# Two graph-convolution layers on one core: z2's operands ahead of one sum, and one sum behind the last multiplication

## The chip, the cores and the metric

The kernel runs on one core of one Trainium2 chip. The metric is the device time of the whole program in microseconds (us); lower is better. Engines are named TensorE (PE, its weight loads PEld), VectorE (DVE), ScalarE (ACT), GpSimd (POOL) and SyncE (SP). L423 is line 423 of the kernel before.

## The reference, cut to what matters

Eight batches of 2048 nodes with 64 features go through two residual graph layers over one adjacency matrix `adj`. Layer 0 has weights of each node's own, made from a 16-wide embedding:

```python
w = einsum('nd,dkio->nkio', embedding, weight)        # D = 16, K = 3
b = einsum('nd,do->no', embedding, bias)
As = [I, A, 2 A @ A - I]
x_g = einsum('knm,bmc->bnkc', stack(As), x)
out = einsum('bnki,nkio->bno', x_g, w) + b
x = layernorm(x + out)
```

Layer 1 uses powers of the same matrix with one weight for all nodes, `x = layernorm(x + concat(x, Ax, (2AA-I)x, ...) @ W + bias)`. All inputs and outputs are float32.

## The kernel before, in words

**Stages.** `pattern` treats `adj` as a pattern of zeros times a factor per row. Two hops of layer 0 come first (`hop_x`, then `seven_products`, which does a block product in seven instead of eight half-size products). They leave z0 (the features), z1 (one hop) and z2 (two hops), each as 16 tiles of 128 nodes by 512 columns (8 batches of 64 features). Then comes the stage of the change: the loop of L897 over the 16 tiles, in which layer 0's node-wise weights are applied. Behind it `run(third + ...)` (L1097) does layer 1's hops.

**One tile of layer 0.** `mix0` (L412) makes eight *pieces*, (u, h) for u in 0 to 3 (a pair of batches) and h in 0 and 1 (half of the 16 embedding dimensions). `product` gives each piece 18 matmuls (L423) into one double bank of PSUM: three inputs (z0, z1, z2) times three operand parts, on two halves of the rows. Each of the inputs is split into three float32r operands: "high" (a ScalarE copy, L327), "low" (source minus high, VectorE L329), and a third, mixed one (VectorE L332 when `quick`, else ScalarE L334 and GpSimd L335). z2's operands of the *following* tile are made by `of_second` in this tile: its first `next` is high, the second low, the third the mixed operand.

The product of a piece must then be multiplied by the node's embedding values and summed over the 8 dimensions of its half. There are three ways:
- kind "D": VectorE multiplies out of PSUM (L439) into `aside`, of which there is one buffer; a VectorE sum over it (L468) follows later as ("reduce", u, h);
- kind "R": ScalarE multiplies in eight steps (L452), and VectorE sums as ("reduce", u, h);
- kind "P": ScalarE multiplies, and GpSimd adds in three steps (L457, "sum") and once more (L461, "add").

("add_reduced", h, us) is GpSimd's addition of finished sums to the tile (L472). A piece's double bank comes free when its multiplications are done.

**The order.** From L751 on, VectorE, ScalarE and GpSimd run in the order in which the program writes their instructions (`ordered`). That order is written out by hand: `at[n]` lists what is issued ahead of piece n, and `pieces` says which piece is of which kind. In tiles 0 to 14 the pieces are

```python
pieces = [(2, 0, "R"), (0, 1, "D"), (3, 0, "R"), (0, 0, "P"), (1, 1, "D"), (1, 0, "P"), (2, 1, "D"), (3, 1, "D")]
```

Into the same lists go the norm of the tile before (`scaled_to_unit`, L374: squares on ScalarE L368, sum on VectorE L379, five small GpSimd steps L385 to L389 and the scaling L390), the transpositions of the next z1 tile ("pt") and of the last h ("pt", copied by L321), and, after the pieces, the projection of the tile before (`project`, L485: matmuls "pu" L493, ScalarE copies L502).

**PSUM.** `bank` hands out four double banks under one tag, for pieces, transpositions, projections and, behind the last tile, for the four accumulators "accT" of layer 1's first hop (L691). By the addresses in the compiled program of before, the first piece of a tile gets the bank of the last tile's piece (2,1), and the transposition behind it that of piece (3,1). Of the accumulators, the first product's two get the banks of the last tile's pieces (2,1) and (3,1).

**The last tile** has another order. It also prepares layer 1's first steps by `early`: `y_high` is a ScalarE copy (L249), `y_low` a VectorE subtraction (L253), `operands` a ScalarE copy of the matrix part (L684).

Of the kernel before, what the change touches and what calls it, by code (L numbers as in the profile page):

```python
# [41 lines left out]
def pattern(  # L42
# [275 lines left out]
    def transpose(src, tag, pt=None):  # L318

        tt = xcpool.tile([P, B // 2, P], F32, tag="ln_xc", name=tag)  # L320
        ordered(nc.scalar.copy(by_half(tt), transposed(src, pt)))  # L321
        return tt
# [83 lines left out]
    def begin_sum(t):  # L406
        ordered(nc.gpsimd.tensor_tensor(bc(0, t), bc(0, t), ebias[:, t : t + 1, :].to_broadcast([P, B, C]), ALU.add))
# [77 lines left out]
    def project(t, hT, pus=None):  # L485


        for g in range(2):
            pm = bank("pu") if pus is None else pus[g]
            for i in range(2):  # L490
                for j in range(2):
                    q = slice(j * C, (j + 1) * C)
                    nc.tensor.matmul(  # L493
                        pm[:, j, i * 3 * C : (i + 1) * 3 * C], lhsT=hT[q, 2 * g + i, :], rhs=v[q],
                        start=True, stop=True,
                    )
            got = pm[:, :, : 6 * C].rearrange("p j (i k c) -> p j i k c", i=2, k=3)

            order = ["p (i j) c -> p j i c", "p (j i) c -> p j i c", "p (j i) c -> p j i c"]
            to = [bc(k, t)[:, 4 * g : 4 * g + 4, :].rearrange(order[k], j=2) for k in range(3)]  # L500
            for k in range(3):
                ordered(nc.scalar.copy(to[k], got[:, :, :, 2 - k, :]))  # L502
# [242 lines left out]
    def times_r(t):  # L745
        to = z2[:, t, :].rearrange("p (j n) -> p j n", n=P)
        r = rrow[:, t * P : (t + 1) * P].unsqueeze(1).to_broadcast([P, B // 2, P])
        ordered(nc.gpsimd.tensor_tensor(to, to, r, ALU.mult))
# [9 lines left out]
    def operands(t, quick=False):  # L758

        xt = work2.tile([P, B // 2, P], F32, tag="t0", name="xt")  # L760
        load(nc.sync, xt, xT[t])
        tt = [None] * 3

        def begin(k, src, quick):
            where, tag = ((rawp, "raw"), (spool, "s"))[k != 2]
            high = hpool.tile([P, B // 2, P], F32R, tag="hl", name="hl")
            pair = where.tile([P, 2, B // 2, P], F32R, tag=tag, name="parts")
            tt[k] = [high, pair[:, 0], pair[:, 1]]
            return parts(src, tt[k], by_half if k == 1 else lambda to: to, quick)

        def of_x():
            yield from begin(0, xt, True)

        def of_hop(pt=None):
            yield from begin(1, transposed(z[1][t], pt), quick)

        def of_second():
            yield from begin(2, by_pair(z[2][t]), True)

        return tt, of_x(), of_hop, of_second()  # L780
# [100 lines left out]
    def early(i, *kinds):  # L881

        got = third_got.setdefault(i, {})
        for lead, part in sorted(third[i], key=lambda part: -part[0]):
            if part.__name__ in kinds:
                part(got)
        third[i] = [part for part in third[i] if part[1].__name__ not in kinds]

    def go(it):
        return lambda: next(it)  # L890
# [5 lines left out]
    everything = range(B // 2)  # L896
    for t in range(NT):  # L897
        got, last = {}, t == NT - 1
        at = [[] for _ in range(9)]
        n1, n2, root, n3 = [lambda: next(norm)] * 4 if t else [nothing] * 4  # L900

        if not last:
            following, of_x, of_hop, of_second = coming
            of_hop = of_hop()
            at[1] += [go(of_x)] * (1 if t else 3)
            at[1] += [n1, lambda: begin_sum(t + 1)]
            if t + 2 < NT:
                at[1] += [lambda: times_r(t + 2)]
            at[1] += [go(of_hop)]
            at[2] += [("reduce", 0, 1), n2, go(of_hop), go(of_hop), ("reduce", 2, 0)]  # L910
            at[3] += [root]
            at[4] += [n3, go(of_second), ("reduce", 3, 0)]
            if t + 2 < NT:
                at[4] += [lambda: got.update(coming=operands(t + 2))]
            at[5] += [("reduce", 1, 1), go(of_second), go(of_second), ("add_reduced", 0, (2, 3))]
            at[7] += [("reduce", 2, 1), ("sum", 0)]
            at[7] += [lambda: got.update(hT=transpose(h, "hT"))] if t else []
            at[8] += [("add", 0, (0, 1)), ("reduce", 3, 1), ("add_reduced", 1, everything)]
            pieces = [(2, 0, "R"), (0, 1, "D"), (3, 0, "R"), (0, 0, "P"), (1, 1, "D"), (1, 0, "P"), (2, 1, "D"), (3, 1, "D")]
        else:  # L920
            at[1] += [n1, n2, root]
            at[2] += [n3, lambda: early(0, "y_high", *s), lambda: early(1, "load_sum")]
            at[3] += [("reduce", 0, 1), ("sum", 0), lambda: early(0, "y_low")]
            at[4] += [lambda: early(1, "y_high", "operands")]
            at[5] += [("reduce", 1, 1), ("reduce", 2, 0), lambda: early(1, "y_low"), ("add", 0, (0, 1))]
            at[6] += [lambda: got.update(hT=transpose(h, "hT")), lambda: early(2, "y_high")]
            at[7] += [("reduce", 2, 1), ("reduce", 3, 0), ("add_reduced", 0, (2, 3)), lambda: early(3, "y_high")]
            at[8] += [("reduce", 3, 1), ("add_reduced", 1, everything), lambda: early(2, "y_low"), lambda: early(3, "y_low")]
            pieces = [(0, 0, "P"), (1, 0, "P"), (0, 1, "D"), (2, 0, "R"), (1, 1, "D"), (3, 0, "R"), (2, 1, "D"), (3, 1, "D")]
        norm_now = mix0(t, tt, at, pieces)  # L930
        if t:
            project(t - 1, got["hT"])
        if "coming" in got:
            coming = got["coming"]
            next(coming[1])
            next(coming[1])
        norm, h = norm_now, z[0][t]
        if not last:
            tt = following
# [427 lines left out]
def gnn_kernel(tc, x, xT, adj, diag, rcols, bias, pack, w0, out):  # L1367
    nc = tc.nc
    with tc.tile_pool(name="flag", bufs=1) as fpool:
        flag = fpool.tile([1, 1], I32, tag="flag", name="flag")  # L1370
        odd = pattern(tc, x, xT, adj, diag, rcols, bias, pack, w0, out, flag)
        with tc.If(odd > 0):
            general(tc, x, adj, bias, pack, w0, out)
# [47 lines left out]
```

## Time and profile before

| what | value |
|---|---|
| median of 3 runs (lowest, highest) | 756.72 us (756.58, 757.08) |
| the profiled execution's own time | 756.74 us |
| its span, first to last instruction | 755.0 us |
| mean granted TensorE clock | 0.997 |
| stage of the change (tiles of layer 0) | 226.5 to 518 us of the span |
| one undisturbed tile on TensorE | 18.33 us |
| VectorE multiplication L439, 64 times | 1.225 us median |
| VectorE sum L468, 96 times | 1.220 us median |
| z2's low L329, 16 times | 0.682 us median |
| third operand L332, 33 times | 0.693 us median, 2.881 the longest |
| GpSimd add L457, the first of three | 2.4 us |

The profile is of one execution. Times in it are microseconds from the start of the span. A timeline row gives start, length, engine, line, operation, what is written and read, shape, and in square brackets how long the engine stood idle before and which engine and line released it. The end of a matmul is modelled: consecutive matmuls overlap, so the distance of two starts is a better measure than a length. A long VectorE row can contain time in which the instruction had been issued and did not run.

### The profile page before, as it was taken

The numbers are of one execution on the slowest core, as the hardware profiler recorded it, in microseconds if no ns is written. First come the engines' busy times: TensorE is split into PE (matmuls) and PEld (weight loads), VectorE is DVE, ScalarE is ACT, GpSimd is POOL, SyncE is SP. The second block draws the span as 40 slices with busy tenths as digits, with TensorE's granted clock in tenths as the row PEclk, the third lists the DMA queues.
The fourth block names the chain that finished last, engine by engine and source line by source line (L and its number), as shares of the span: only waits on it lengthen the run. The fifth ranks groups of instructions, "written<-read, shape, count | busy, mean of one in ns | idle before, by whom it ended". The sixth has DMA issues, their size and how long they took to land.

```text
span 755.0 us, 13518 instructions
## 1 busy us (share of the span) xinstructions
PE 744.3 (99%) x4942; PEld 613.0 (81%) x4942; DVE 618.1 (82%) x965; ACT 453.4 (60%) x1106; POOL 277.9 (37%) x299
## 2 busy tenths in 40 slices
PE   9999999999999999999999999999999999999995
PEld 6887888888888788888888888887788888888885
DVE  6768888999978999999999999979588557778563
ACT  5437444878755777777777777778877662112111
POOL 0001111133253877777777777664000000021430
PEclk9999999999999999999999999999999999999998
DMA  9998987555420000000000000004454454665621
GB/s 322 376 400 282 326 279 278 175 160 168 153 85 15 16 16 16 15 15 17 20 24 15 16 15 1 2 30 127 128 165 142 137 171 138 180 183 167 205 88 47
DMA packets 73691, 96.49 MB, mean 128 GB/s; under 512 B 5009, under 2 KB 48529, under 8 KB 73489
## 3 DMA queue, kind: packets, MB, share of 16 engines
q1 hardware_dynamic: 62208, 76.66, 32.2%
q10 hardware_dynamic: 11408, 18.89, 6.8%
q8 instruction: 41, 0.67, 0.4%
q14 instruction: 34, 0.27, 0.1%
HBM read 76.65 MB, written 18.87 MB: 127 GB/s over the span
## 4 chain that ended last, share of the span: by engine, by line
PE 92%; DVE 5%; issue 1%; POOL 1%; ACT 0%; DVEq 0%; POOLq 0%
PE pm L423 29%; PE accT L697 27%; PE acc L269 15%; PE a L269 10%; PE accT L269 6%; PE pu L493 2%; DVE aside L439 2%; DVE sums L468 1%; PE pt L315 1%; DVE parts L332 1%; PE first L145 1%; PE accT L853 1%; DVE parts L329 1%; ACT aside L452 0%; PE accT L493 0%
## 5 line engine op out<-in xcount | busy, mean ns | idle before, releaser
L697 PE MATMUL accT<-s,hl 128*128 128x512 f32 x896 | 206.1, 391 | 0.4 <-DVE aside L439 0.4
L697 PEld LDWEIGHTS accT<-s,hl 128*128 128x128 f32 x896 | 167.4, 188 | 36.7 <-DVE aside L439 0.9
L452 ACT ACTIVATE aside<-pm,pack_sb 128x128 f32<-128x128 f32 x512 | 140.2, 402 | 40.2 <-PE pm L423 40.2
L423 PE MATMUL pm<-wh,hl 64*128 64x512 f32 x768 | 154.6, 399 | 0.7 <-DVE aside L439 0.7
L423 PE MATMUL pm<-wm,parts 64*128 64x512 f32 x768 | 150.1, 388 | 0.0
L423 PE MATMUL pm<-wl,parts 64*128 64x512 f32 x768 | 149.7, 387 | 0.0
L684 ACT CAST s<-raw 128x1024 fp32r<-128x1024 bf16 x104 | 110.1, 1059 | 37.0 <-ACT hl L249 27.6
L468 DVE TENSOR_REDUCE sums<-aside 128x128 f32<-128x1024 f32 x96 | 115.9, 1210 | 3.2
L269 PE MATMUL acc<-hl,s 128*128 128x512 f32 x512 | 116.9, 390 | 0.0
L269 PEld LDWEIGHTS acc<-hl,s 128*128 128x128 f32 x512 | 95.9, 188 | 20.8 <-DVE z L578 0.9
L249 ACT CAST hl<-z 128x256 fp32r<-128x256 f32 (+1 forms) x96 | 47.8, 516 | 62.8 <-PE acc L269 21.6
L439 DVE TENSOR_TENSOR aside<-pm,pack_sb 128x1024 f32<-128x1024 f32 x64 | 78.3, 1223 | 8.7 <-PE pm L423 6.3
L423 PEld LDWEIGHTS pm<-wm,parts 64*128 64x128 f32 x768 | 71.9, 184 | 15.7
L423 PEld LDWEIGHTS pm<-wh,hl 64*128 64x128 f32 x768 | 72.3, 185 | 15.0 <-DVE aside L439 1.0
L457 POOL TENSOR_TENSOR aside<-aside 128x1024 f32<-128x1024 f32 (+2 forms) x48 | 71.6, 1491 | 32.3 <-ACT aside L452 29.8
L423 PEld LDWEIGHTS pm<-wl,parts 64*128 64x128 f32 x768 | 72.1, 185 | 13.8
L269 PE MATMUL a<-hl,s 128*128 128x512 f32 (+1 forms) x352 | 73.4, 370 | 0.0
L253 DVE TENSOR_TENSOR hl<-z,hl 128x512 fp32r<-128x512 f32 (+1 forms) x96 | 57.8, 610 | 16.6 <-ACT hl L249 7.6
L269 PEld LDWEIGHTS a<-hl,s 128*128 128x128 f32 x352 | 61.9, 188 | 11.3
L403 POOL TENSOR_TENSOR s<-s,part 128x8 f32<-128x8 f32 x16 | 7.0, 440 | 166.9 <-DVE s L402 145.8
L302 POOL TENSOR_TENSOR z<-z,got 128x512 f32<-128x512 f32 x3 | 4.8, 1622 | 144.1 <-ACT got L301 144.1
L368 ACT ACTIVATE sq<-z 128x512 f32<-128x512 f32 x31 | 20.0, 651 | 48.8 <-DVE z L304 46.6
(138 smaller groups left out, 948.4 us busy)
## 6 DMA issues: line engine op xcount, KB each, us to landing
raw<-in_adj SPq DMA_DIRECT2D x58, 512.0 KB, 6.0
raw<-sums_of SPq DMA_DIRECT2D x64, 256.0 KB, 2.9
sums_of<-z ACTq DMA_DIRECT2D x16, 512.0 KB, 6.8
raw<-quarters SPq DMA_DIRECT2D x32, 256.0 KB, 2.7
raw<-in_adj SPq DMA_DIRECT2D x16, 384.0 KB, 3.5
quarters<-seen ACTq DMA_DIRECT2D x16, 256.0 KB, 5.9
xt<-in_xT SPq DMA_DIRECT2D x16, 256.0 KB, 2.7
z<-in_x SPq DMA_DIRECT2D x15, 256.0 KB, 6.7
```

What stands on the lines that cost most here:

```text
L249: ordered(nc.scalar.copy(to[0], src))
L253: ordered(nc.vector.tensor_tensor(to[1], src, to[0], ALU.subtract))
L269: nc.tensor.matmul(accs[i], lhsT=s[:, i * P : (i + 1) * P], rhs=hl[h], start=(first and h == 0), stop=(last and h == 1),)
L368: ordered(nc.scalar.activation(sq, src, AF.Square))
L423: nc.tensor.matmul(pm[:, j], lhsT=tt[k][n][q, u, :], rhs=w_parts[n][k][q, ds, :], start=(k == 0 and n == 0), stop=(k == 2 and n == 2),)
L439: ordered(nc.vector.tensor_tensor(side_by_side(a), got, e, ALU.mult))
L452: ordered(nc.scalar.activation(to[d], got, AF.Copy, scale=emb_sb[:, t, h * DD + d : h * DD + d + 1]))
L457: ordered(nc.gpsimd.tensor_tensor(to, to, more, ALU.add))
L468: ordered(nc.vector.tensor_reduce(to, src, AX.X, ALU.add))
L493: nc.tensor.matmul(pm[:, j, i * 3 * C : (i + 1) * 3 * C], lhsT=hT[q, 2 * g + i, :], rhs=v[q], start=True, stop=True,)
L684: ordered(nc.scalar.copy(s, got["raw"]))
L697: nc.tensor.matmul(acc[i][:, c], lhsT=hl[h][:, i * P : (i + 1) * P], rhs=S[:, c * 512 : (c + 1) * 512], start=(kk == 0 and h == 0), stop=( ...
```

## The change

In tiles 0 to 14 the low half and the third operand of the following z2 tile are issued ahead of the sum of piece (1,1); before, they stood behind it. In the last tile the sum of piece (3,0), and GpSimd's addition of the two finished sums, move from ahead of the last multiplication (piece (3,1)) to behind it; step 2's `y_low` goes ahead of them, directly behind that multiplication. No instruction is added, removed or resized, and no DMA is moved.

```diff
@@ -912,7 +912,7 @@
             at[4] += [n3, go(of_second), ("reduce", 3, 0)]
             if t + 2 < NT:
                 at[4] += [lambda: got.update(coming=operands(t + 2))]
-            at[5] += [("reduce", 1, 1), go(of_second), go(of_second), ("add_reduced", 0, (2, 3))]
+            at[5] += [go(of_second), go(of_second), ("reduce", 1, 1), ("add_reduced", 0, (2, 3))]
             at[7] += [("reduce", 2, 1), ("sum", 0)]
@@ -924,8 +924,11 @@
             at[6] += [lambda: got.update(hT=transpose(h, "hT")), lambda: early(2, "y_high")]
-            at[7] += [("reduce", 2, 1), ("reduce", 3, 0), ("add_reduced", 0, (2, 3)), lambda: early(3, "y_high")]
-            at[8] += [("reduce", 3, 1), ("add_reduced", 1, everything), lambda: early(2, "y_low"), lambda: early(3, "y_low")]
+            at[7] += [("reduce", 2, 1), lambda: early(3, "y_high")]
+            at[8] += [
+                lambda: early(2, "y_low"), ("reduce", 3, 0), ("add_reduced", 0, (2, 3)),
+                ("reduce", 3, 1), ("add_reduced", 1, everything), lambda: early(3, "y_low"),
+            ]
```

## The prediction

> **What bounds the kernel now.** I read four views: the page's busy shares, the list of waits for TensorE, the timelines of single engines around each wait, and the tile-to-tile distance on TensorE. D(u,h) stands for VectorE's multiplication of piece (u,h) (L439), R(u,h) for its sum (L468), "low" for L329, "third" for the third operand of z2 (L332).
>
> From the page:
>
> ```profile
> PE 744.3 (99%) x4942; PEld 613.0 (81%) x4942; DVE 618.1 (82%) x965; ACT 453.4 (60%) x1106; POOL 277.9 (37%) x299
> ```
>
> TensorE is the bound, 99% of the span of 755.0. A reorder on VectorE can pay only where TensorE stands still, and that is this short list (us in total, times, longest):
>
> ```profile
> PE first L145 <- DVE part L146: 1.3, 1, 1.3
> PE pm L423 <- DVE aside L439: 0.7, 1, 0.7
> PE accT L697 <- DVE aside L439: 0.4, 1, 0.4
> PE pt L315 <- DVE aside L439: 0.3, 1, 0.3
> ```
>
> The first is the start of the kernel. The other three lie where the change works. TensorE behind tile 1 (start, length, line, form, idle before):
>
> ```profile
> 260.27 1.46 PE L493 MATMUL pu<-v,hT 64*128 64x192 f32 x16
> 262.45 0.50 PE L423 MATMUL pm<-wh,hl 64*128 64x512 f32 x2 [0.72 <-DVE aside L439]
> 265.03 0.46 PE L315 MATMUL pt<-ident,z 64*128 64x64 f32 x8 [0.25 <-DVE aside L439]
> ```
>
> and VectorE, then GpSimd, in the same microseconds:
>
> ```profile
> 255.28 1.21 DVE L439 TENSOR_TENSOR aside<-pm,pack_sb 128x1024 f32<-128x1024 f32 x1
> 256.52 1.22 DVE L468 TENSOR_REDUCE sums<-aside 128x128 f32<-128x1024 f32 x1
> 257.66 0.68 DVE L329 TENSOR_TENSOR parts<-z,hl 128x512 fp32r<-128x512 f32 x1
> 258.38 2.88 DVE L332 SCALAR_TENSOR_TENSOR parts<-hl,parts 128x512 fp32r<-128x512 f32 x1
> 261.18 1.21 DVE L439 TENSOR_TENSOR aside<-pm,pack_sb 128x1024 f32<-128x1024 f32 x1
> ```
>
> ```profile
> 255.87 1.04 POOL L390 TENSOR_TENSOR z<-z,ln_r 128x512 f32<-128x512 f32 x1
> 256.87 0.74 POOL L472 TENSOR_TENSOR z<-z,sums 128x256 f32<-128x256 f32 x1
> ```
>
> ```profile
> 258.31 2.40 POOL L457 TENSOR_TENSOR aside<-aside 128x1024 f32<-128x1024 f32 x1 [0.69 <-ACT aside L452]
> ```
>
> The third operand takes 2.88 us where its median is 0.693. It starts 0.07 behind GpSimd's L457 and ends at 261.26, that is 0.55 behind L457's end (258.31 + 2.40 = 260.71). D(2,1) comes only then, ends at 262.39, and TensorE starts at 262.45; D(3,1) ends at 264.98, TensorE starts at 265.03.
>
> The last tile, VectorE and TensorE:
>
> ```profile
> 516.23 1.22 DVE L439 TENSOR_TENSOR aside<-pm,pack_sb 128x1024 f32<-128x1024 f32 x1
> 517.49 2.35 DVE L468 TENSOR_REDUCE sums<-aside 128x128 f32<-128x1024 f32 x2
> 519.75 1.22 DVE L439 TENSOR_TENSOR aside<-pm,pack_sb 128x1024 f32<-128x1024 f32 x1
> ```
>
> ```profile
> 519.39 1.21 PE L697 MATMUL accT<-s,hl 128*128 128x512 f32 x4
> 521.02 1.66 PE L697 MATMUL accT<-s,hl 128*128 128x512 f32 x6 [0.41 <-DVE aside L439]
> ```
>
> Both R(2,1) and R(3,0) stand ahead of D(3,1), which ends at 520.97; half of the next hop's accumulators need its bank.
>
> **What these waits really cost.** Idle times count from modelled ends of overlapping matmuls, so I use starts. The projection (L493) starts at 260.27 in tile 1, 280.03 in tile 2, 298.37 in tile 3. Tile 2 to 3 is 18.34, the undisturbed distance (18.33 further on); 1 to 2 is 19.76. The two waits cost 19.76 - 18.34 = **1.42 us**, not 0.97. At the accumulators, the fourth matmul starts at 519.39 + 1.21 - 0.39 = 520.21; matmuls follow each other in about 0.23, so the fifth was due at 520.44 and came at 521.02: 0.58. A burst's first interval is about 0.11 longer than the others and is paid a second time: **0.69 us**.
>
> **Part one, tile 1.** Nothing is added or removed; low (0.68) and third (0.69) go ahead of R(1,1) (1.22). No DMA and no instruction of another queue moves; SyncE and ScalarE keep their order, and low's input (L327, 254.82 to 255.55) is ready. What changes is what GpSimd does at that moment. Low is now issued at 256.52, with L390 running to 256.91. The nearest rows for its cost are low and third of the next x: low starts at 283.24 under L461 (282.76 to 283.50) and ends at 284.05, third ends at 285.76, and L472 (283.58, 1.63 long) ends at 285.21. Each VectorE step ends 0.55 behind the GpSimd step in its way; L472, itself held by low, ends 1.16 behind low instead of taking 1.29. So they take turns, and a waiting step loses about 0.13 of its own length. Then:
> - low ends 256.91 + 0.55 = 257.46; L472 follows, 0.74 - 0.13 = 0.61, to 258.07; third ends 258.07 + 0.55 = 258.62, not 261.26.
> - R(1,1) starts 258.54, D(2,1) 1.1 later at 259.65 and ends 260.87. TensorE was due at 260.27 + 1.16 (projection to the next piece in an undisturbed tile, 298.37 to 299.53) = 261.43: margin 0.5.
> - R(2,1), then D(3,1) at 262.0, ending 263.25; TensorE's transposition is due 2.16 behind 261.43, at 263.6: margin 0.3.
>
> All 1.42 us go. The Trainium skill ("SBUF — State Buffer", "SBUF: two separate sides") says that VectorE with two SBUF inputs and GpSimd share a pair of ports as an exclusive lock: the first to start has it for its whole instruction, the other fully blocks. That rule speaks against the move: it puts low behind L390 and third behind L472 in *every* tile. With whole instructions behind each other the sum is 256.91 + 0.68 + 0.74 = 258.33, which is 0.02 after L457 appears at 258.31; by the rows it is 258.07, 0.24 before. I take the rows, and one more row says that a waiting VectorE goes first: L407 started on GpSimd at 285.17, before L472 ended at 285.21, and third still ended at 285.76. Bounds of this part: -1.42 and, if L457 gets in first, third ends at 261.26 again with R(1,1) now behind it: D(2,1) ends about 1.1 later than before, D(3,1) 0.9, so +0.9.
>
> **The other tiles.** In tile 3: D(1,1) ends 293.33, L390 runs 292.54 to 293.58, L472 would start 293.55, L457 comes at 296.40. New: low ends 294.13, L472 294.74, third 295.29 (before: 295.91), R(1,1) ends about 296.4, D(2,1) starts 296.46 instead of 296.19: 0.27 late. It ends 297.7; its bank is wanted at 299.53. D(3,1) is 0.19 late and ends 300.2; wanted at 301.75. R(3,1) is 0.19 late and fits into the 0.33 that VectorE waits for ScalarE's L327 ahead of the next low. So the 0.8 us of new blocking per tile is covered by waits of 0.28, 0.1 and 0.33, and by 1.5 us of slack at the banks: cost 0. With that cover gone it would be 13 times up to 0.8, some 10 us. GpSimd's L472 slips by 0.45, and 1.66 us of idling before L457 cover it. R(1,1)'s reader on GpSimd comes only at the end of the tile. In tile 0 GpSimd idles from 239.11 to 241.63, over both moved steps: 0. Tile 2 is where VectorE was still behind; it starts that tile 1.7 earlier against TensorE's 1.42, gives back 0.8, and keeps about 1 us at the banks: 0.
>
> **Part two, last tile.** R(3,0) and GpSimd's L472 on it go behind D(3,1). D(3,1)'s product has its last matmul at 517.77 + 0.39 = 518.16; VectorE is free at 517.49 + 1.13 = 518.62. So D(3,1) ends at 519.84, 0.6 before the fifth accumulator matmul is due (520.44). If the accumulators fall on another bank in the new order, the next candidates are those of the projection, copied by ScalarE from 518.86 in six steps of 0.27: three are done by 519.8, all at 520.6. So -0.69, with bounds -0.69 and about -0.4. What is late next: the same VectorE work in another order, with the y low of step 2 now first (needed near 523), that of step 3 at about 522.8 (needed near 525). GpSimd's second L472 waits for R(3,1) and ends near 523.9 instead of 523.7; ScalarE is busy until 524.22 before it squares that result. The transpositions of this tile's h, at 531.22 before, come 0.69 closer to the norm's end (529.64); 0.9 us remain. Behind that TensorE runs without a gap to 747, so nothing else sets the end.
>
> **Sum.** Profiled execution 756.74 (span 755.0 and 1.74 around it): 756.74 - 1.42 - 0.69 = 754.63. The median of the runs shown is 756.72, the same within 0.02. I predict 754.6, 0.28% faster. A measurement of this kernel can tell about 0.2%, or 1.5 us, from no change, so both parts are needed to cross it.
>
> **Rivals.**
> - Only one part works: -1.42 (755.3), if the accumulators wait on; or -0.69 (756.0), if tile 1's stall moves to the next bank. For: margins of 0.3 to 0.6 us. Against: the starts and ends above leave no other late engine. Chance 0.20.
> - No change (756.7): the stall is taken up later, where VectorE or a load is due anyway. Against it: TensorE has no other wait from 265 to 747. Chance 0.06.
> - Slower: third gets its port behind L457, decided at 258.31 in tile 1 and 296.40 in tile 3. In tile 1 alone it gives +0.9 - 0.69, so 756.9 (chance 0.05). If it happened in all tiles, third would end 296.40 + 2.41 + 0.55 = 299.36, D(2,1) at about 301.6 against 299.53, D(3,1) at 304.0 against 301.75: over 2 us in each of 14 tiles, about 787. For that L472 must end 1.66 us later than worked out. With lesser forms, such as the cover per tile failing, chance 0.07.
> - Both parts as worked out: 754.3 to 755.0, chance 0.62.
>
> Faster by over 0.2% needs 755.2 or less: the forecast and a little of the partial case, 0.65. Within 0.2%: 0.28. Slower: 0.07. The range runs from 754.2 (the scatter of 0.3 of the runs before) to 756.2 (either part alone).
>
> **What would show it.** Right: no wait of pm or pt for L439 near 262 and 265, none of accT near 518; third at about 1.13 us in tile 1 and later, low at 0.94 in tile 1 and about 0.76 later; projections 1 to 2 at 18.3; D(3,1) of the last tile right behind one sum. Wrong: a third of near 2.9 us in any tile, or a new wait of TensorE on L439 that repeats every 18.3 us.

## The result, and the profile after

The changed kernel takes 753.5 us (median of 5 runs, 752.74 to 753.68) against 756.72. The ratio is 0.9955, with a 95% interval of 0.994 to 0.997: 3.2 us or 0.4% faster. The prediction was 754.6, and its range ended at 754.2. The profiled execution's own time is 753.22 (span 751.3), 3.52 less than the one of before. The granted clock is 0.999 against 0.997; further down, two kernels with one order and clocks of 0.996 and 0.999 have the same middle (518.13), so the clock does not make the difference. Behind the diff, line numbers are higher by 3.

The busy line of the page and the whole list of waits for TensorE, after:

```profile
PE 743.0 (99%) x4942; PEld 613.1 (82%) x4942; DVE 622.4 (83%) x965; ACT 453.0 (60%) x1106; POOL 284.3 (38%) x299
```

```profile
PE first L145 <- DVE part L146: 1.3, 1, 1.3
```

All three waits for L439 are gone, and none has come in their place. GpSimd is busy 6.4 us longer and VectorE 4.3; neither is seen by TensorE. Tile 1 after, VectorE, then GpSimd (start, length, line, form):

```profile
255.64 1.05 DVE L329 TENSOR_TENSOR parts<-z,hl 128x512 fp32r<-128x512 f32 x1
256.73 1.11 DVE L332 SCALAR_TENSOR_TENSOR parts<-hl,parts 128x512 fp32r<-128x512 f32 x1
257.77 1.21 DVE L468 TENSOR_REDUCE sums<-aside 128x128 f32<-128x1024 f32 x1
259.08 1.23 DVE L439 TENSOR_TENSOR aside<-pm,pack_sb 128x1024 f32<-128x1024 f32 x1
```

```profile
255.10 1.04 POOL L390 TENSOR_TENSOR z<-z,ln_r 128x512 f32<-128x512 f32 x1
256.11 1.19 POOL L472 TENSOR_TENSOR z<-z,sums 128x256 f32<-128x256 f32 x1
257.71 2.41 POOL L457 TENSOR_TENSOR aside<-aside 128x1024 f32<-128x1024 f32 x1 [0.42 <-ACT aside L452]
```

Low, L472 and third take turns: low ends at 256.69, 0.55 behind L390; L472 at 257.30, 0.61 behind low; third at 257.84, 0.54 behind L472. Third takes 1.11 instead of 2.88 us. D(2,1) ends at 260.31, and TensorE wants its bank 1.17 behind the projection that starts at 259.67, at 260.84. In the last tile, VectorE and TensorE:

```profile
515.50 1.22 DVE L468 TENSOR_REDUCE sums<-aside 128x128 f32<-128x1024 f32 x1
516.82 1.23 DVE L439 TENSOR_TENSOR aside<-pm,pack_sb 128x1024 f32<-128x1024 f32 x1
517.96 0.42 DVE L253 TENSOR_TENSOR hl<-z,hl 128x256 fp32r<-128x256 f32 x1
```

```profile
517.42 2.83 PE L697 MATMUL accT<-s,hl 128*128 128x512 f32 x11
```

One sum stands ahead of D(3,1), and the eleven accumulator matmuls run in one piece.

**Where 3.5 us went.** I cut the span in three at TensorE's records: start (up to the first piece of tile 0), middle (from there to the last matmul's start), end (from there to the span's end). "Projections 1 to 2" is the distance that the prediction used. "Last packet" is when the last packet of the output lands, counted from the start of VectorE's last step (which comes 2.65 behind the last matmul's start; 2.95 in kernels with 1222 instructions), and the last column how many VectorE instructions the trace holds, stand-alone waits and branches included. These columns, and the times of single packets below, come from the trace's own lists of instructions and packets. Kernels that the next section introduces are in the same table. Most recorded expectations count the end from the start of VectorE's last step, 2.65 less than here, and a middle that is about 0.2 longer.

| kernel | start | middle | end | projections 1 to 2 | last packet | VectorE instructions |
|---|---|---|---|---|---|---|
| before | 226.45 | 520.28 | 8.23 | 19.76 | 3.19 | 1221 |
| before, three blank lines | 226.29 | 520.27 | 8.56 | 19.75 | 3.53 | 1221 |
| part two alone | 225.51 | 519.58 | 8.45 | 19.75 | 3.41 | 1221 |
| part one alone | 225.90 | 518.84 | 7.44 | 18.31 | 2.39 | 1236 |
| **after** | 225.86 | 518.21 | 7.27 | 18.33 | 2.17 | 1236 |
| after, again | 226.02 | 518.13 | 7.62 | 18.29 | 2.57 | 1236 |
| part one, tile 1 only | 225.62 | 519.01 | 8.11 | 18.46 | 2.77 | 1222 |
| part one, all but tile 1 | 226.22 | 518.89 | 7.40 | 18.34 | 2.36 | 1235 |
| part one from tile 2 | 226.59 | 520.28 | 7.31 | 19.76 | 2.26 | 1234 |
| part one, tile 0 only | 227.06 | 518.89 | 8.19 | 18.34 | 2.82 | 1222 |
| after, list 128 longer than before | 226.81 | 518.13 | 8.58 | 18.29 | 3.53 | 1349 |

The middle is 2.07 shorter in the first profile after and 2.15 in the second; the prediction had 2.11. The start is 0.59 shorter in this pair, but it holds nothing that the change touches, and it lies between 225.5 and 227.1 in these executions without regard to the kernel. What the prediction did not have is the **end**: 0.96 shorter.

### The profile page after: what moved, and what is told of

It reads as the page before. It is cut to its first block, busy times and chain, and to the rows that moved or that the text cites. A ratio compares the mean times of both kernels' runs of the same rounds, so it can differ in the third digit from the quotient of the medians.

```text
span 751.3 us, 13533 instructions
## 1 busy us (share of the span) xinstructions
PE 743.0 (99%) x4942; PEld 613.1 (82%) x4942; DVE 622.4 (83%) x965; ACT 453.0 (60%) x1106; POOL 284.3 (38%) x299
## 4 chain that ended last, share of the span: by engine, by line
PE 99%; DVE 0%; ACT 0%; issue 0%; DVEq 0%
PE pm L423 35%; PE accT L697 27%; PE acc L269 15%; PE a L269 10%; PE accT L269 6%; PE pu L493 3%; PE pt L315 1%; PE accT L853 1%; PE first L145 1%; PE accT L493 0%; PE accT L155 0%; PE accT L315 0%; ACT sq L1041 0%; DVE z L304 0%; DVE got L1046 0%
## 5 line engine op out<-in xcount | busy, mean ns | idle before, releaser
L439 DVE TENSOR_TENSOR aside<-pm,pack_sb 128x1024 f32<-128x1024 f32 x64 | 78.3, 1224 | 6.9 <-PE pm L423 2.9
L457 POOL TENSOR_TENSOR aside<-aside 128x1024 f32<-128x1024 f32 (+2 forms) x48 | 71.0, 1479 | 26.2 <-ACT aside L452 23.7
```

Source lines behind the costliest of these rows:

```text
L439: ordered(nc.vector.tensor_tensor(side_by_side(a), got, e, ALU.mult))
L457: ordered(nc.gpsimd.tensor_tensor(to, to, more, ALU.add))
```

## The experiments

My theory at first: the two waits give 2.1, and the rest is either scatter of the start and of single executions (first rival), or something that the steady tiles gain (second rival), or the layout of the program (third rival).

**First set: the parts (before: 756.77, 33 runs, 755.97 to 758.14).** The kernel before with three blank lines put in, so that it has the changed kernel's line numbers:

> The kernel before with three blank lines, the same instructions. It asks what an execution of the same program varies by outside of the changed stage. Theory (each part gives what the starts on TensorE say, 1.42 and 0.69, and the rest of the measured 3.2 is variation in the first stage and in the last transfer): 756.7 within 0.3, but with the first piece of tile 0 anywhere from 225.9 to 226.6, and 4.1 to 5.3 us from the end of the last VectorE step to the end of the span. Rival (the changed program has a shorter start and tail of its own): first piece again at 226.5, last stretch again at 5.2, within 0.1.

Measured 757.01 (13 runs), ratio 0.9999 [0.999, 1.0007]. The lines do nothing. Single executions of before differ by over 2 us, more than the 0.5 of the runs first shown.

Part one alone, then part two alone:

```diff
-            at[5] += [("reduce", 1, 1), go(of_second), go(of_second), ("add_reduced", 0, (2, 3))]
+            at[5] += [go(of_second), go(of_second), ("reduce", 1, 1), ("add_reduced", 0, (2, 3))]
```

> Only the order in tiles 0 to 14 changed. Theory: the distance of the projections of tiles 1 and 2 falls from 19.76 to 18.34, the wait at the accumulators stays at 0.4, so 1.42 less: 755.3, plus or minus what the start and the last transfer vary by. Rival (part one is worth more than its 1.42, for instance in later tiles): 754.2, with TensorE's stretch from the first piece to the last product shorter by more than 1.5.

Measured 754.12 (5 runs), ratio 0.9964 [0.995, 0.9977]: -2.65.

```diff
-            at[7] += [("reduce", 2, 1), ("reduce", 3, 0), ("add_reduced", 0, (2, 3)), lambda: early(3, "y_high")]
-            at[8] += [("reduce", 3, 1), ("add_reduced", 1, everything), lambda: early(2, "y_low"), lambda: early(3, "y_low")]
+            at[7] += [("reduce", 2, 1), lambda: early(3, "y_high")]
+            at[8] += [
+                lambda: early(2, "y_low"), ("reduce", 3, 0), ("add_reduced", 0, (2, 3)),
+                ("reduce", 3, 1), ("add_reduced", 1, everything), lambda: early(3, "y_low"),
+            ]
```

> Only the order in the last tile changed. Theory: the two waits behind tile 1 stay (0.72 and 0.25), the one at the accumulators goes: 0.69 less, 756.0, plus or minus start and last transfer. Rival (part two is worth the missing 1.1 too): 755.0, with less time between the last tile and the last product than 0.69 below before.

Measured 756.18 (21 runs), ratio 0.999 [0.9984, 0.9997]: -0.59. The changed kernel once more, beside them:

> The changed kernel once more, for a second trace of it. Theory: the stretch from tile 0's first piece to the last product is again 2.1 shorter than before, while the start and the last transfer fall anew; time 752.7 to 754.7. Rival (start and tail are properties of the changed program): first piece again at 225.9 and last stretch at 4.1, time 753.5 within 0.2.

Measured 753.68 (5 runs), ratio 0.9958 [0.9945, 0.9972]: -3.09. The parts add up (2.65 + 0.59 = 3.24). In the middle stretch part one gives 520.28 - 518.84 = 1.44 and part two 0.70, as worked out (1.42 and 0.69). The whole surplus is part one's, and it lies in the end: 7.44 there, 8.45 with part two alone. That ends the second rival, and the first as the reason for the surplus.

**What part one does to the end.** The section on the change says that no instruction is added. The page's first line of before, and then that of after, say otherwise:

```profile
span 755.0 us, 13518 instructions
```

```profile
span 751.3 us, 13533 instructions
```

There are 15 more. The rows of the multiplication's line, before and after, say what they are (count, duration, first and last start):

```profile
L439 DVEq EVENT_SEMAPHORE  x34: 21/21/21, 235.5 to 518.7; - x34
```

```profile
L439 DVEq EVENT_SEMAPHORE  x49: 21/21/21, 234.9 to 516.8; - x49
```

Each of tiles 0 to 14 has one more stand-alone wait. With R(1,1) directly ahead of D(2,1), which overwrites what R(1,1) reads, the compiled program has D(2,1) wait for two semaphores, VectorE's own and TensorE's, and the wait for VectorE's own takes an instruction of its own. With low and third in between, it waits for TensorE's alone. The kernels of the table that have the new order in 1, 13 or 14 tiles hold 1, 13 or 14 instructions more. A wait of 21 ns is no cost; but it shifts VectorE's list. Packets of 8 KB (queue q14) bring instructions. Some of them keep step with VectorE's list, each 128 instructions or so: in before they begin when VectorE is at its 575th, 702nd, 832nd, 958th, 1091st and 1216th instruction, and in the changed kernel within 3 of these places, up to 12 us earlier in time. In before the last of them falls on the last five of the 1221 instructions. DMA in the 2.4 us that begin 0.9 behind the start of VectorE's last step, before (GB/s in 40 slices of 0.06 us; packets by queue):

```profile
GB/s 0 0 137 0 0 0 85 324 290 375 324 307 256 154 69 0 137 137 0 0 0 0 17 0 17 0 17 0 0 17 0 0 17 0 0 17 17 17 0 0
q1 hardware_dynamic: 144, 0.13, 18.5%
q14 instruction: 4, 0.03, 6.0%
```

The same stretch after:

```profile
GB/s 0 0 137 0 0 0 102 188 273 341 307 307 308 171 51 17 34 137 51 154 17 0 0 0 0 0 0 0 0 0 0 0 0 0 0 0 0 0 0 0
q1 hardware_dynamic: 144, 0.13, 17.8%
q14 instruction: 3, 0.02, 3.7%
```

The 144 packets of q1 are the last 128 KB of the output. In both kernels over 120 of them have landed by 1.8. Both have an instruction packet that begins at 1.02 or 1.04. In before, a second one follows it at 1.35 and takes 0.89, to 2.24 (two more begin at 1.91 to 2.09 in both, when most of the output has landed); nine output packets, a sixteenth of 144, begin only at 2.22 and trickle in one by one to 3.19. After, the fetch for the same place in the list came 2.4 ahead of that last step, and the nine end at 2.17. The span ends 2.4 behind the last packet in both. What differs is that second packet. So the new theory: the place of VectorE's last fetch sets the last 1 us; its rival is that the new order of the tiles itself does.

**Second set: which tiles, and the list alone (before: 757.26, 12 runs).** Part one in tile 1 only, then in all tiles but tile 1 (`t != 1` in the same place):

```diff
-            at[5] += [("reduce", 1, 1), go(of_second), go(of_second), ("add_reduced", 0, (2, 3))]
+            at[5] += [go(of_second), go(of_second), ("reduce", 1, 1)] if t == 1 else [("reduce", 1, 1), go(of_second), go(of_second)]
+            at[5] += [("add_reduced", 0, (2, 3))]
```

> The new order in tile 1 alone, the last tile as before; VectorE's list of instructions is 1 longer than before (a wait of its own), not 15. Theory (tile 1 holds the whole gain of TensorE in part one; the shorter end comes from where VectorE's list of instructions lies against its fetches of 8 KB): first piece to the last tile's end on TensorE 1.42 shorter, the end behind the last VectorE step stays at 5.6 to 5.9; time 755.3. Rival (the short end belongs to the earlier operands or to an earlier finish): end at 4.6 to 5.0; time 754.2.

Measured 755.04 (8 runs), ratio 0.9975 [0.9965, 0.9986]. The tile that had the stall is enough to remove it but for 0.13 (projections 1 to 2 at 18.46), and the end stays at 8.11.

> The new order in tiles 0 and 2 to 14, tile 1 and the last tile as before; VectorE's list is 14 longer. Theory: the waits of 0.7 and 0.25 behind tile 1 stay, TensorE's middle is that of before (520.5 from the first piece to the last product's use), but the end is short, 4.6 to 5.0; time 755.7. Rival (end tied to TensorE's earlier finish or to tile 1): nothing changes, 756.8.

Measured 754.0 (5 runs), ratio 0.9962 [0.9948, 0.9975]. A miss: the end is short, as expected, but the stall behind tile 1 is gone too, although tile 1 has its old order. Its third, on VectorE, and L457, on GpSimd:

```profile
258.00 0.69 DVE L332 SCALAR_TENSOR_TENSOR parts<-hl,parts 128x512 fp32r<-128x512 f32 x1
```

```profile
258.08 2.87 POOL L457 TENSOR_TENSOR aside<-aside 128x1024 f32<-128x1024 f32 x1 [0.85 <-ACT aside L452]
```

Third now comes 0.08 ahead of L457, where it was 0.07 behind, and L457 pays (2.87 instead of 2.40). Fourteen tiles were left as candidates for that; the third set splits them.

To move the list without the order, 15 settings of a new 32-byte tile at the start of the kernel before, and in the changed kernel 115 (two per step of a hop in layer 1), which make its list 128 longer than before's:

```diff
+    pad = keep.tile([P, B], F32, tag="pad", name="pad")
...
+        for _ in range(15):
+            tc.keep_in_program_order(nc.vector.memset(pad, 0.0))
```

> The kernel before with 15 more VectorE memsets of 8 columns, in the first microseconds, in which VectorE waits for the first load; no order changed. Theory (fetches): the middle as before, the end 4.6 to 5.0 instead of 5.6 to 5.9, a fetch of 8 KB at about 2 us ahead of the last VectorE step instead of 1.3 to 1.9 behind it; time 755.8, so 15 instructions more make it faster by 1.0. Rival (the end is short because of the operands' order): as before, 756.8 or a little more.

> The changed kernel with 115 more VectorE memsets of 8 columns, two behind each step of layer 1's first hop (two waits fall away, so that the list is 113 longer than that of the changed kernel and 128, or 8 KB, longer than that of before). Theory (fetches of 8 KB that hold 128 instructions): TensorE's middle as in the changed kernel, since VectorE has room in that hop, but the end is that of before again, 5.6 to 5.9; time 754.6. Rival: the end stays short, 753.6; if VectorE has no room, TensorE shows new waits in the hop and the time is above 755.

Measured 767.23 (ratio 1.0137 [1.0122, 1.0153]) and 768.08 (1.0145 [1.0129, 1.016]). The ends moved as the fetch theory said, 7.14 for the kernel before and 8.73 for the changed one. But something else made every hop slower by far more, so the totals say nothing of it: inconclusive.

**Third set (before: 756.97, 30 runs, 755.75 to 758.39).** Part one from tile 2 on (`t > 1`), and in tile 0 only (`t == 0`):

> The new order in tiles 2 to 14 only; tiles 0, 1 and the last as before; VectorE's list is 13 longer than before. In the run with all tiles but tile 1 the wait behind tile 1 was gone too, so my account of it (tile 1's own order) was too narrow. Theory now: third and GpSimd's first addition meet within 0.1 us in tile 1, and either tile 0's or tile 1's order decides who is first. With both as before: third at 2.9 in tile 1, waits of 0.7 and 0.25, TensorE's middle 520.5, only the short end (4.6 to 5.0): 755.8. Rival (the later tiles do it): waits gone, 754.3.

Measured 756.01 (18 runs), ratio 0.9986 [0.9978, 0.9993]: -0.96. All waits are back:

```profile
PE pm L423 <- DVE aside L439: 0.7, 1, 0.7
PE accT L697 <- DVE aside L439: 0.4, 1, 0.4
PE pt L315 <- DVE aside L439: 0.3, 1, 0.3
```

The middle is 520.28, exactly that of before, with 13 tiles in the new order: these tiles give nothing and take nothing. What is left is the end, 7.31 with 1234 instructions.

> The new order in tile 0 alone; VectorE's list is 1 longer. Theory now: in tile 0 third no longer overlaps GpSimd's first addition, whose chain starts 0.15 earlier, low of the next x escapes GpSimd's L461, and third of tile 1 comes 0.1 ahead of GpSimd instead of 0.07 behind: 0.69 long, no wait behind tile 1, middle 519.1; the end as with the order in tile 1 alone (8.1 from the last matmul); time 755.1. Rival (tile 1's own order is needed): third 2.9, time 756.8.

Measured 755.6 (11 runs), ratio 0.9981 [0.9972, 0.999]: -1.37. One tile earlier, the order of tile 0 alone removes tile 1's stall. Tile 1 of that kernel, VectorE and GpSimd:

```profile
258.83 0.69 DVE L332 SCALAR_TENSOR_TENSOR parts<-hl,parts 128x512 fp32r<-128x512 f32 x1
```

```profile
258.92 2.86 POOL L457 TENSOR_TENSOR aside<-aside 128x1024 f32<-128x1024 f32 x1 [0.87 <-ACT aside L452]
```

The reason lies in tile 0. GpSimd's three L457 and the low of the following x, before, then with the new order in tile 0:

```profile
241.63 4.76 POOL L457 TENSOR_TENSOR aside<-aside 128x1024 f32<-128x1024 f32 x3 [2.53 <-ACT aside L452]
246.83 0.94 DVE L329 TENSOR_TENSOR parts<-xt,hl 128x512 fp32r<-128x512 f32 x1
```

```profile
242.24 4.60 POOL L457 TENSOR_TENSOR aside<-aside 128x1024 f32<-128x1024 f32 x3 [2.52 <-ACT aside L452]
247.50 0.71 DVE L329 TENSOR_TENSOR parts<-xt,hl 128x512 fp32r<-128x512 f32 x1
```

In before, third (241.25, 0.69 long) overlapped L457, which took 4.76; with third out of the way it takes 4.60. L461 then starts at 4.68 behind L457's start instead of 4.84, and the low of the following x, which had been held by L461, takes 0.71 instead of 0.94. That is how 0.16 us reaches the next tile and decides who comes first there: counted from tile 0's first piece, tile 1's third starts at 31.77 instead of 31.93, and L457 at 31.86 in both.

The kernel before with one setting of the new tile, to see what slowed the two inconclusive runs:

```diff
+    pad = keep.tile([P, B], F32, tag="pad", name="pad")
...
+        tc.keep_in_program_order(nc.vector.memset(pad, 0.0))
```

> The kernel before with one more SBUF tile of 8 columns (32 bytes a partition, one memset), which moves the work buffers behind it from byte 111072 to 111104. No order is changed. Theory (in the two runs with more memsets the moved buffers, not the memsets, cost some 10 us): matmuls of 396 ns instead of 391 in the first hop, 119.5 us for it instead of 116.3, time 767. Rival (the memsets cost it): 756.8.

Measured 767.98, ratio 1.0141 [1.0126, 1.0157]. The new tile takes 32 bytes of each partition ahead of the work buffers. The kernels with the order of tile 0 or 1 alone have as many VectorE instructions (1222) and are not slower, so the tile is the reason, not the setting. The matmuls of the first hop, before and here:

```profile
L269 PE MATMUL acc<-hl,s 128*128 128x512 f32 x512 | 116.9, 390 | 0.0
```

```profile
L271 PE MATMUL acc<-hl,s 128*128 128x512 f32 x512 | 119.8, 396 | 0.0
```

So I repeated the disputed run without a new tile: the changed kernel, with 115 settings of an existing tile to the value that it has.

```diff
+                if s == 0:
+                    for _ in range(5 if p == 0 and kk == 0 else 2):
+                        ordered(nc.vector.memset(part, 1.0 / C))
```

> The changed kernel with two more VectorE memsets behind each step of layer 1's first hop, into a tile that exists, so that no buffer moves; VectorE's list is 128 instructions (8 KB) longer than that of before, so that it lies against its fetches as before. Theory: TensorE's middle as in the changed kernel (518.4), the end as before (5.6 to 5.9): 754.6, which is the prediction's sum. Rival (the end belongs to the order): 753.6; or VectorE has no room in that hop: above 755.

Measured 754.96 (7 runs), ratio 0.9971 [0.9959, 0.9982]: -2.01. The waits for TensorE are those of the changed kernel, and its middle too (518.13); the end is 8.58. The same stretch of DMA, 0.9 behind the start of VectorE's last step:

```profile
q14 instruction: 4, 0.03, 6.6%
q8 instruction: 1, 0.02, 2.5%
```

The fetch is back at 1.60, and the last output packet lands at 3.53. (The 16 KB packet of q8 lies at the same place in the second profile of after, from 0.90 on, whose end is short.) With the same order and only the list's length changed, 1 us returns, and the 2.01 that remain are close to the predicted 2.11. The kernel before with 15 settings is the converse: the old order, the short end. That settles the fetch's place against the order of the tiles.

In the eight kernels with 1221, 1222 or 1349 instructions, the second packet ends 1.87 to 2.75 behind the start of VectorE's last step, and the last output packet lands 0.90 to 1.14 behind that end. In the six with 1234 to 1236 there is no such second packet, and the last output packet lands at 2.02 to 2.57.

**A pause in VectorE's own list.** VectorE also pauses for about 0.3 us at a fixed place of its list, the 1216th instruction, and 128 later in the kernels with 1349. In before, that is the branch behind the last step, which comes 0.32 instead of 0.01 behind that step's start. In the changed kernel it is a load of a flag, 0.39 instead of 0.04 behind the start of the step ahead of it, with time to spare. In the kernels with 1222 it is the last step itself. Before, then with the new order in tile 0 only:

```profile
749.38 0.42 DVE L1043 TENSOR_TENSOR got<-z,ln_r 128x256 f32<-128x256 f32 x1
```

```profile
748.90 0.42 DVE L1044 TENSOR_TENSOR got<-z,ln_r 128x256 f32<-128x256 f32 x1 [0.33 <-DVE ln_r L360]
```

This is why the last step of these kernels comes 2.95 instead of 2.65 behind the last matmul's start. The second packet begins 1.03 to 1.48 behind the place. That the fetch is what makes VectorE pause fits this, but the trace does not name the cause.

## Why the prediction was right and wrong

- **The two waits' cost: right.** 2.11 was predicted from starts of projections and matmuls, 2.07 and 2.15 were measured; the idle times of the list of waits (0.72 + 0.25 + 0.41 = 1.38) would have given two thirds of it.
- **Turn-taking of VectorE and GpSimd: right, by the rows.** From L390's end to third's end 1.71 was predicted and 1.70 measured. The rule of the Trainium skill ("SBUF — State Buffer", "SBUF: two separate sides"), that a holder keeps the ports for its whole instruction, would have given 0.68 + 0.74 + 0.69 = 2.11, if each ran its full length behind the other. The exclusion is as the page says (third, 0.07 behind L457, took 2.88), but the step that waits ends 0.54 to 0.61 behind the holder and not its full 0.68 to 0.74. Part of its work may be behind it when its turn comes; no run shows that.
- **Margins in tile 1: right in sign.** D(2,1) had 0.53 (predicted 0.5), D(3,1) ends at 262.89 against 263.03, 0.14 (predicted 0.3). In the last tile D(3,1) is 0.2 later than worked out, with 0.4 left of 0.6.
- **Other tiles at 0: right in total.** Tile 2 to 3 stays at 18.33, and the kernel with the new order from tile 2 on has the middle of before to 0.01.
- **"In tile 0 ... 0": wrong in detail.** That tile's order alone removes the stall. The two causes remove one and the same wait, so the sum didn't show it. The total for part one would have come out with either order alone. Had I asked what 0.07 us in tile 0 could do, I'd have seen that the stall hung on so little.
- **The step that failed: "Behind that TensorE runs without a gap to 747, so nothing else sets the end", and with it the sum "756.74 - 1.42 - 0.69".** The change adds 15 waits to VectorE's list, the list's last 8 KB fetch moves off the last output transfer, and the end is 0.96 shorter in this pair of profiles (7.1 to 7.6 against 8.2 to 8.7 over all that have one list or the other). That term was missing: 754.63 - 0.96 = 753.67, against 753.5 and 753.68. I had taken "no instruction is added" from the source; waits are added by the compiler, and only the compiled list shows them. The Trainium skill ("Runtime: NRT & Kernel Launch", "Instruction fetch mechanics") says that crossing from one 16 KiB block of instructions to the next is "mostly hidden"; the packets of this trace's queue are 8 KB. At the end of this kernel it is not: the second packet delays the last output packet by about 1 us. VectorE's pause of 0.3, which may belong to the same crossing, delays the last step in the kernels with 1222 instructions.
- **The rivals: none came.** No wait moved to the next bank, none appeared later, and L457 came 0.41 behind L472's end in tile 1, where 0.24 had been worked out.
- **The range: too narrow below.** It took 0.3 for the scatter below. The 75 further runs of before spread over 2.6 us. Even so it was the missing term, not the scatter, that moved the median out of the range.

**What stays open.** That the nine late packets wait for the same DMA engine as the fetch fits their number (9 of 144 on one of 16) and their time (2.22 against the fetch's end at 2.24), but the trace doesn't name a packet's engine. It doesn't name the engine that a packet of instructions is for either: that the second packet is VectorE's is read from its place in VectorE's list, and from the list's length, which decides whether it is there. Why 32 bytes slow the matmuls is open as well; that it is the buffers' place was not tested apart from the tile.

## What to carry to other kernels

Cost a wait by the distance of starts to the next undisturbed repetition, not by its idle time, and ask how little would have avoided it: a collision lost by 0.07 us can be undone by a change of 0.16 a tile earlier. Where a reorder changes which semaphores an instruction waits for, it changes the length of the engine's list; look at what is fetched while the last output is written. A kernel that reordering makes 1 us faster by its last fetch can lose that again with the next unrelated edit, so compare two orders over a stretch of the span, not only by the total.

## What the runs showed of the hardware that was not expected

- A second 8 KB instruction packet among the last 128 KB of output makes the last output packets land at 3.2 to 3.7 us instead of 2.0 to 2.6, and the span ends 8.2 to 8.7 us behind the last matmul's start instead of 7.1 to 7.6 (five kernels with 1221 or 1349 VectorE instructions against six with 1234 to 1236; the three with 1222 lie between, at 2.8 to 2.9 and 8.1 to 8.2).
- At the 1216th instruction of its list VectorE pauses for about 0.3 us. Where that is its last step, the step starts after 0.33 us of idling (0.32 in the other two such kernels), against 0.03 to 0.04 elsewhere.
- A new tile of 32 bytes in each partition ahead of the work buffers makes the first hop's matmuls 396 instead of 390 ns long and the kernel 1.4% slower, at a like granted clock (0.998 against 0.997).
- Of two steps of VectorE and GpSimd that collide, the one that comes 0.07 to 0.09 us earlier pays nothing. The other pays 2.19 (third behind L457, 2.88 instead of 0.69) or 0.46 (L457 behind third, 2.86 instead of 2.40).
